# A two-layer attention kernel whose first q and k are projected from centred values and scaled as they leave PSUM

## The chip, the cores and the metric

The kernel runs on one core of a Trainium2 chip. The metric is the device time of one execution in microseconds (us), the median of several. The core has five engines that run side by side, each taking its own instructions in order: TensorE (PE, matrix products; its weight loads are shown as PEld), VectorE (DVE), ScalarE (ACT), GpSimd (POOL) and SyncE (SP, which here only issues DMAs). Products land in PSUM, [...]which this kernel holds as four tiles of two banks with the tags a, b, c and d. A tile is reused only when its readers are done.

## The reference

Sixteen images of 256 channels on a 32 by 32 grid go through two layers. Each layer normalises in 16 groups and adds the attention of the normalised image to the image:

```python
def _gn(v, G=16, eps=1e-5):
    B_, H_, W_, C_ = v.shape
    g = v.reshape(B_, H_, W_, G, C_ // G)
    m = jnp.mean(g, axis=(1, 2, 4), keepdims=True)
    s = jnp.var(g, axis=(1, 2, 4), keepdims=True)
    return ((g - m) / jnp.sqrt(s + eps)).reshape(v.shape)

...
    q = proj(Wq, bq)
    k = proj(Wk, bk)
    v = proj(Wv, bv)
    sim = jnp.einsum('bhdi,bhdj->bhij', q, k)
    rel = (rel_h + rel_w).reshape(heads, d, n)
    qpos = jnp.einsum('hdi,bhdj->bhij', rel, q)
    attn = jax.nn.softmax(sim + qpos, axis=-1)
    out = jnp.einsum('bhdn,bhmn->bhdm', v, attn)
...
x = x + _L0_conv_ref(_gn(x), ...)
x = x + _L1_conv_ref(_gn(x), ...)
```

There are 4 heads of 64 channels and 1024 positions. The groups lie along the last axis of the grid: a group is two neighbouring columns of every row of every channel. A group's mean and its 1/sqrt(variance), called rstd below, are therefore the same for all channels and differ by position only. Since a projection sums over channels, a factor that depends on the position alone can be applied to the projection's result as well as to its input.

## The kernel before

**Units and blocks.** A unit is one image in one layer, so there are 32. A unit has four blocks: two pairs of heads (`pr`) by two halves of the query positions (`half`). A block computes the scores of both heads of its pair as eight tiles `ps` of 128 keys by 2 x 512 queries (L385), their exponentials `p` (L394, on ACT), the running sum `acc` of those for the softmax's denominator (L403, L405, on DVE), and the product with the values, `po` (L419). Before PE adds the scores to a tile, DVE writes the position term there from `abt` (a "seed", L349).

**What stands between.** The function `block` writes out the order of work by hand, and a manual schedule keeps it, so each engine executes its instructions in the order in which the code names them. Between its own scores a block runs pieces of the unit's second pair and of the next unit (`prepare`): values (L298), q and k (L268), positions (L326). A projection or value product is made in two stretches; between the two stands a small write on POOL (L166) that waits for the first and releases the second.

**Normalisation ahead.** While unit u runs, the statistics of unit u + 2 are gathered on ACT in 16 groups each of sums (L190 with Identity) and squares (L190 with Square), and unit u + 1 is normalised in 16 ACT instructions (`norm_apply`, L248). A product with the constant matrix `avg` adds a statistic over the partitions: `norm_mean` and `norm_var` by four small products (L209). rstd is a power, taken on POOL (L237).

**The beginning.** Before the first block no earlier work is there to hide in. SP loads image 0, Wq and Wk of layer 0 (`raw0`), image 1, both Wv (`raw1`), Wq and Wk of layer 1 (`raw2`), the small tables and image 2. Weights are transposed on PE (L126) and copied out by ACT (L137). For image 0, DVE sums by group (L858), PE averages (L868), ACT negates the mean (L870), DVE writes the centred image `xn` (L875), ACT and DVE share the squares (L190, L888, L889), PE averages (L894), DVE adds epsilon (L896), POOL takes the power (L901), and DVE and ACT share the scaling of `xn` (L928, L925). Then PE makes q and k (L268), ACT adds the bias on the way out of PSUM (L279), PE makes the positions. Unit 1's mean and squares are made in between, all before block 0; its rstd is ready during block 0, whose `norm_apply` calls begin with it. Unit 2's sums run on ACT in blocks 0 and 1 (`norm_sums`).

**The end.** The last block makes the sums for its softmax on PE into a PSUM tile `pd`. DVE takes the reciprocal (L827), ACT copies the sums to SBUF (L829), two DMAs bring one row of each head into a table (L831), and DVE and PE reduce that table to a flag that says whether all sums were in range. The copy's buffer `d` comes from the pool of the exponentials:

```python
    d = ppool.tile([P, 2, HALF], F32, tag="p", name=f"d_{n + 1}")[:, 0, :]
    nc.scalar.copy(d, pd)
```

The four PSUM tags go round in a list `ring`, which starts as b, c, a, d.

Of the kernel before, what the change touches and what calls it, by code (L numbers as in the profile page):

```python
# [9 lines left out]
F32 = mybir.dt.float32  # L10
# [7 lines left out]
P = 128  # L18
# [34 lines left out]
def fast_path(ctx, tc, sh, x, layers, out, W, den_all, token, good, flag):  # L53
# [55 lines left out]
    def load_raw(name, parts):  # L109

        raw = ppool.tile([P, 2, HALF], F32, tag="p", name=name)
        for a, (l, part) in enumerate(parts):
            nc.sync.dma_start(
                raw[:, a, :].rearrange("p (oc c) -> p oc c", c=C),
                layers[l][part].rearrange("(oc p) c -> p oc c", p=P),
            )
        return raw, parts
# [74 lines left out]
        )  # L192

    def norm_sums(u, gs):
        if u not in reds:
            reds[u] = small.tile([P, G], F32, tag="red", name=f"red_{u}")
        for g in gs:
            of_group(u, g, AF.Identity, reds[u])
# [27 lines left out]
    def norm_squares(u, gs):  # L226
        for g in gs:
            of_group(u, g, AF.Square, sums[u], bias=negs[u][:, g : g + 1])
# [14 lines left out]
        return out_of_psum  # L243

    def norm_apply(u, gs):
        rstd, shift = rss[u]
        for g in gs:
            nc.scalar.activation(  # L248
                grouped(xns[u], g),
                grouped(xt[units[u][0]], g),  # L250
                AF.Identity,
                bias=shift[:, g : g + 1],
                scale=rstd[:, g : g + 1],
            )
# [142 lines left out]
    def add_up(blk, j):  # L397
        u, pr, half = blk
        if j == 0:
            return  # L400
        if j == 1:
            accs[blk] = apool.tile([P, 2, HALF], F32, tag="acc", name=f"acc_{u}_{pr}_{half}")
            nc.vector.tensor_tensor(accs[blk], probs[blk, 0], probs[blk, 1], ALU.add)  # L403
        else:
            nc.vector.tensor_tensor(accs[blk], accs[blk], probs[blk, j], ALU.add)  # L405
# [179 lines left out]
    BPU = CC * NH  # L585

    pos = {}
    ring = ["b", "c", "a", "d"]

    def nothing(*_):  # L590
        return None
# [1 line left out]
    def prepare(u, b):  # L593
# [22 lines left out]
            positions(u, 0, psum2(y, f"pa_{u}_0")),  # L616
        )

    def block(n):
        blk = blocks[n]  # L620
        u, b = divmod(n, BPU)
# [17 lines left out]
        if previous:  # L639
# [4 lines left out]
                add_last(previous)  # L644
            else:
                add_up(previous, 7)
        for j in range(1, 4):
            scores(blk, j)
        (first, first_out), (second, second_out) = prepare(u, b)
        first(0)  # L650
        if b == 0 and one:
            norm_apply(u + 1, range(0, 1))
        if b == 1 and two:
            norm_sums(u + 2, range(9, 11))
        seed(blk, 4, f1)
        scores(blk, 4)
        add_up(blk, 1)
        if b == 0 and one:
            norm_apply(u + 1, range(1, 5))
        if b == 1 and two:  # L660
            norm_sums(u + 2, range(11, 12))
        if b == 2 and two:
            norm_squares(u + 2, range(0, 5))
        second(0)
        if half == 1:
            second_out()
# [16 lines left out]
        if previous and folded:  # L683
            stack_up(previous)
        add_up(blk, 2)
        if half == 0:
            second(1)
            second_out()
# [10 lines left out]
            seed(after, 0, f0)  # L699
        if n in check:  # L700
            next(checks)
        if b == 0 and one:
            norm_apply(u + 1, range(5, 9))
        if b == 0 and two:
            norm_sums(u + 2, range(0, 2))
        if b == 1 and two:
            norm_sums(u + 2, range(12, G))
        if b == 1 and one:
            norm_apply(u + 1, range(9, 11))
        if b == 2 and two:  # L710
            norm_squares(u + 2, range(5, 11))
        po = psum2(ring[3], f"po_{n}")
        values_of_p = attend(blk, po)
        values_of_p(0)
# [4 lines left out]
                mean_out = norm_var(u + 2, filled(f1, f"pm_{n}", EPS / 2))  # L719
        if after:  # L720
            scores(after, 0)
        values_of_p.word()
        if stacked:
            fold_stack(*stacked, R // 2)
# [5 lines left out]
            add_up(blk, 5)  # L730
        if before:
            finish(*before)
        if two and half == 1:
            mean_out()
        if stacked:
            fold_stack(*stacked, R // 4)
# [5 lines left out]
                seed(after, j, ring[j % 3])  # L742
        if summed:
            reciprocals(*summed)
        if b == 0 and two:
            norm_sums(u + 2, range(2, 9))
        if b == 1 and one:
            norm_apply(u + 1, range(11, G))
        if b == 2 and two:
            norm_squares(u + 2, range(11, G))  # L750
        values_of_p(1)
        take_out(blk, po)
        pos[n] = po
# [8 lines left out]
    def block_without_pieces(n, half):  # L762
# [62 lines left out]
        values_of_p(1)  # L825
        rden = rdens[u, pr][:, HALF:]
        nc.vector.reciprocal(rden, pd)  # L827
        d = ppool.tile([P, 2, HALF], F32, tag="p", name=f"d_{n + 1}")[:, 0, :]
        nc.scalar.copy(d, pd)  # L829
        for hs in QUARTERS:  # L830
            nc.sync.dma_start(den_all[hs, n, :], d[hs.start : hs.start + 1, :])  # L831
# [7 lines left out]

    load_x(0)  # L840
    raw0 = load_raw("raw0", [(0, "Wq"), (0, "Wk")])
    load_x(1)
    raw1 = load_raw("raw1", [(0, "Wv"), (1, "Wv")])
    raw2 = load_raw("raw2", [(1, "Wq"), (1, "Wk")])
    W.load_rest(nc.sync, 0)
    load_x(2)
# [2 lines left out]
    def by_group(t, g0=0, g1=G):  # L849
        return t.rearrange("p c (w g t) -> p (c w) g t", g=G, t=GT)[:, :, g0:g1, :]  # L850

    def spread(t, g0=0, g1=G):
        return (
            t[:, g0:g1].unsqueeze(1).unsqueeze(3).to_broadcast([P, CC * sh.W, g1 - g0, GT])
        )

    def reduced(u, cc):
        nc.vector.tensor_reduce(  # L858
            reds[u][:, cc, :],
            xt[units[u][0]][:, cc, :].rearrange("p (w g t) -> p g w t", g=G, t=GT),  # L860
            AX.XY,
            ALU.add,
        )

    def first_mean(u, pm):
        red = reds.pop(u)
        for cc in range(CC):
            nc.tensor.matmul(pm, W.avg, red[:, cc, :], start=(cc == 0), stop=(cc == CC - 1))  # L868
        negs[u] = small.tile([P, G], F32, tag="neg", name=f"neg_{u}")
        nc.scalar.mul(negs[u], pm, -1.0)  # L870
        sums[u] = small.tile([P, G], F32, tag="sum", name=f"sum_{u}")
        xns[u] = gnpool.tile([P, CC, N], F32, tag="gn", name=f"xn_{u}")

    def centred(u, g0, g1):
        nc.vector.tensor_tensor(  # L875
            by_group(xns[u], g0, g1),
            by_group(xt[units[u][0]], g0, g1),
            spread(negs[u], g0, g1),
            ALU.add,
        )  # L880

    def rest_of_squares(u, g0):

        sq = ppool.tile([P, 2, HALF], F32, tag="p", name=f"first_sq_{u}")
        sq = sq.rearrange("p a n -> p (a n)")[:, : CC * sh.W * (G - g0) * GT].rearrange(
            "p (w g t) -> p w g t", g=G - g0, t=GT
        )
        nc.vector.tensor_tensor(sq, by_group(xns[u], g0), by_group(xns[u], g0), ALU.mult)  # L888
        nc.vector.tensor_reduce(  # L889
            sums[u][:, g0:], sq.rearrange("p w g t -> p g w t"), AX.XY, ALU.add  # L890
        )

    def first_var(u, pm):
        nc.tensor.matmul(pm, W.avg, sums.pop(u), start=True, stop=True)  # L894
        var = small.tile([P, G], F32, tag="var", name=f"var_{u}")
        nc.vector.tensor_scalar(var, pm, EPS, None, ALU.add)  # L896
        return var

    def first_rstd(u, var):
        rstd = small.tile([P, G], F32, tag="rstd", name=f"rstd_{u}")  # L900
        nc.gpsimd.tensor_tensor(rstd, var, W.mhalf[:, :G], ALU.pow)  # L901
        return rstd

    for u in range(2):
        reds[u] = small.tile([P, CC, G], F32, tag="first_red", name=f"first_red_{u}")
    G1, G2 = G // 2 + 2, G // 4
    pm0 = psum2("c", "pm_0")
    for cc in range(CC):
        reduced(0, cc)
    first_mean(0, pm0[:, 0, :G])  # L910
    transposed("a", *raw0)
    norm_squares(0, range(G1))
    centred(0, 0, G)
    rest_of_squares(0, G1)
    rstd0 = first_rstd(0, first_var(0, pm0[:, 1, :G]))
    taken(raw0[1])
    transposed("b", *raw1)
    taken(raw1[1])
    pm1 = psum2("d", "pm_1")
    for cc in range(CC):  # L920
        reduced(1, cc)
    first_mean(1, pm1[:, 0, :G])
    transposed("a", *raw2)
    for g in range(G2):
        nc.scalar.activation(  # L925
            grouped(xns[0], g), grouped(xns[0], g), AF.Identity, scale=rstd0[:, g : g + 1]
        )
    nc.vector.tensor_tensor(  # L928
        by_group(xns[0], G2), by_group(xns[0], G2), spread(rstd0, G2), ALU.mult
    )  # L930
    taken(raw2[1])
    norm_squares(1, range(0, G // 2))
    centred(1, G // 2, G)
    rest_of_squares(1, G // 2)
    (q, q_out), (k, k_out) = (
        project(0, 0, which, psum2(tag, f"p{which}_0_0")) for which, tag in (("q", "b"), ("k", "c"))
    )
    q(0)
    k(0)
    q(1)  # L940
    q_out()
    k(1)
    k_out()
    ab, ab_out = positions(0, 0, psum2("a", "pa_0_0"))
    ab(0)
    ab_out()
    var1 = first_var(1, pm1[:, 1, :G])
    for j in range(3):
        seed(blocks[0], j, ring[j])
    v, v_out = values(0, 0, psum2("d", "pv_0_0"))  # L950
    v(0)
    scores(blocks[0], 0)
    v(1)
    v_out()
    seed(blocks[0], 3, ring[0])
    rstd1 = first_rstd(1, var1)
    shift1 = small.tile([P, G], F32, tag="nshift", name="nshift_1")
    nc.vector.tensor_tensor(shift1, negs.pop(1), rstd1, ALU.mult)
    rss[1] = (rstd1, shift1)
    for n in range(len(blocks)):  # L960
        block(n)

# [279 lines left out]
```

## Time and profile before

| what | value |
|---|---|
| median of three runs | 2537.84 us (2536.82 to 2538.13) |
| the profiled execution's own time | 2537.8 us |
| its span in the profile | 2535.9 us |
| PE busy | 2512.9 us, 99% of the span |
| DVE busy | 2267.8 us, 89% |
| ACT busy | 1949.0 us, 77% |
| POOL busy | 834.1 us, 33% |

The span reaches from the first to the last instruction recorded; 1.9 us of the execution's time lie around it. A row of the profile names the line of the code, the engine, and the tiles written and read. "x16" counts instructions; a matrix product in 32-bit floats shows as two records. Times within the trace count from the start of the span.

### The profile page before, as it was taken

Reading aid. Unit: us, or ns where it says so; the run is one execution under the profiler, and the core shown is the slowest. Engines: PE = TensorE matmul, PEld = TensorE weight load, DVE = VectorE, ACT = ScalarE, POOL = GpSimd, SP = SyncE. Lnnn points to the kernel's source line nnn. Section 1 sums busy time; section 2 is a strip of 40 time slices with the busy share of each in tenths; the row PEclk is TensorE's granted clock in tenths of the full one; section 3 lists DMA queues with packets and bytes.
Section 4 is the critical chain, followed back from the end, with each engine's and each line's share of the span. In section 5 each row is a group of like instructions: output and inputs, shape, how many; then the busy total and the mean of one; then the engine's idle time right before and its main releaser. Section 6 shows DMA issues by size and latency. Waiting matters only on the chain.

```text
span 2535.9 us, 85952 instructions
## 1 busy us (share of the span) xinstructions
PE 2512.9 (99%) x37462; PEld 1332.5 (53%) x37462; DVE 2267.8 (89%) x2133; ACT 1949.0 (77%) x3876; POOL 834.1 (33%) x1195
## 2 busy tenths in 40 slices
PE   8999999999999999999999999999999999999998
PEld 4555555555555555555555555555555555555554
DVE  6898998989989989899899899998998999989997
ACT  6778777787777887777877778877778777787654
POOL 1333333323333233333233332333323333323320
PEclk9999999999999999999999999999999999999999
DMA  3344443544444445444444444444454444444442
GB/s 90 74 79 75 87 87 67 101 96 93 96 90 104 80 76 101 88 84 95 92 88 94 79 97 81 85 104 90 87 112 81 90 79 84 80 84 77 95 81 69
DMA packets 119841, 221.57 MB, mean 87 GB/s; under 512 B 53913, under 2 KB 55449, under 8 KB 119457
## 3 DMA queue, kind: packets, MB, share of 16 engines
q0 software_dynamic: 53712, 130.10, 31.4%
q1 hardware_dynamic: 65744, 85.90, 12.0%
q8 instruction: 295, 4.83, 0.8%
q14 instruction: 90, 0.73, 0.1%
HBM read 51.78 MB, written 17.30 MB: 27 GB/s over the span
## 4 chain that ended last, share of the span: by engine, by line
PE 97%; DVE 1%; DMA 1%; POOL 1%; issue 1%; SPq 0%; ACT 0%; POOLq 0%; DVEq 0%; ACTq 0%
PE ps L385 34%; PE po L419 34%; PE pk L268 9%; PE pv L298 9%; PE pq L268 9%; PE pa L326 2%; DMA stack<-stack 0%; DMA den_all<-d 0%; PE pm L209 0%; DMA x<-in_x_dram 0%; DVE acc L405 0%; DVE rden L827 0%; POOL rstd L237 0%; POOL rstd L901 0%; POOL stack L460 0%
## 5 line engine op out<-in xcount | busy, mean ns | idle before, releaser
L349 DVE TENSOR_TENSOR ps<-abt 128x1024 f32<-128x1024 f32 x1018 | 1228.8, 1230 | 230.3 <-ACT p L394 144.3
L394 ACT ACTIVATE p<-ps,shift 128x1024 f32<-128x1024 f32 x1024 | 1091.3, 1114 | 335.4 <-PE ps L385 335.4
L385 PE MATMUL ps<-q,k 64*64 64x512 f32 x8192 | 985.9, 590 | 0.0
L419 PE MATMUL po<-p,v 64*64 64x256 f32 x16384 | 930.5, 376 | 0.0
L419 PEld LDWEIGHTS po<-p,v 64*64 64x64 f32 x16384 | 629.1, 133 | 364.3 <-issue 77.2
L405 DVE TENSOR_TENSOR acc<-acc,p 128x1024 f32<-128x1024 f32 x643 | 780.4, 1214 | 8.2 <-ACT p L394 1.4
L385 PEld LDWEIGHTS ps<-q,k 64*64 64x64 f32 x8192 | 306.6, 133 | 397.9 <-issue 274.9
L166 POOL MEMSET token<- 1x1 f32 x320 | 36.2, 113 | 1033.5 <-PE po L419 469.9
L465 POOL DMA_DIRECT2D stack<-stack x310 | 255.0, 823 | 196.0 <-DMA stack<-stack 109.4
L298 PE MATMUL pv<-Wv,xn 64*64 64x256 f32 x4096 | 244.3, 376 | 0.6 <-POOL token L166 0.3
L268 PE MATMUL pq<-xn,Wq 64*64 64x512 f32 x2048 | 243.8, 591 | 0.3 <-DVE xn L928 0.3
L268 PE MATMUL pk<-xn,Wk 64*64 64x512 f32 x2048 | 242.8, 589 | 0.0
L460 POOL DMA_DIRECT2D stack<-acc x248 | 221.6, 1075 | 41.6 <-issue 30.0
L248 ACT ACTIVATE xn<-x,nshift,rstd 128x128 f32<-128x128 f32 x496 | 210.3, 496 | 1.1 <-POOL nshift L239 1.1
L298 PEld LDWEIGHTS pv<-Wv,xn 64*64 64x64 f32 x4096 | 153.5, 133 | 102.7 <-issue 51.6
L436 POOL DMA_DIRECT2D acc<-p x124 | 118.8, 958 | 247.3 <-ACT od L480 162.3
L190 ACT ACTIVATE junk<-x,neg 128x128 f32<-128x128 f32 x498 | 195.2, 400 | 0.0
L480 ACT COPY od<-po 128x512 f32<-128x512 f32 x127 | 74.3, 585 | 114.9 <-PE po L419 114.9
L403 DVE TENSOR_TENSOR acc<-p,p 128x1024 f32<-128x1024 f32 x128 | 155.8, 1217 | 0.0
L441 POOL DMA_DIRECT2D acc<-acc x124 | 106.0, 855 | 148.3 <-DMA acc<-p 139.3
L268 PEld LDWEIGHTS pq<-xn,Wq 64*64 64x64 f32 x2048 | 78.6, 134 | 142.1 <-issue 133.2
L190 ACT ACTIVATE junk<-x 128x128 f32<-128x128 f32 x480 | 145.0, 311 | 0.0
(75 smaller groups left out, 1124.5 us busy)
## 6 DMA issues: line engine op xcount, KB each, us to landing
acc<-p POOLq DMA_DIRECT2D x124, 512.0 KB, 5.7
rden<-rd SPq DMA_DIRECT2D x126, 256.0 KB, 6.0
acc<-acc POOLq DMA_DIRECT2D x124, 256.0 KB, 3.6
x<-in_x_dram SPq DMA_DIRECT2D x32, 512.0 KB, 4.3
stack<-acc SPq DMA_DIRECT2D x248, 64.0 KB, 2.1
stack<-acc POOLq DMA_DIRECT2D x248, 64.0 KB, 3.0
out_dram<-x SPq DMA_DIRECT2D x31, 512.0 KB, 3.8
stack<-stack POOLq DMA_DIRECT2D x62, 128.0 KB, 4.2
```

Source lines behind the costliest of these rows:

```text
L190: nc.scalar.activation(junk, grouped(xt[units[u][0]], g), func, accum_out=into[:, g : g + 1], **bias)
L248: nc.scalar.activation(grouped(xns[u], g), grouped(xt[units[u][0]], g), AF.Identity, bias=shift[:, g : g + 1], scale=rstd[:, g : g + 1],)
L268: yield nc.tensor.matmul(pk[c, nh, :], w[l][rs, cc, c0 : c0 + D], xns[u][rs, cc, nh * HALF : (nh + 1) * HALF], start=(t == 0 and cc == 0), ...
L298: yield nc.tensor.matmul(pv[c, a, i, :], xns[u][rs, cc, j0 : j0 + D], W.wv[l][rs, cc, :], start=(t == 0 and cc == 0 and i == 0), stop=(t = ...
L349: nc.vector.tensor_tensor(ps.rearrange("p h (w y) -> p h w y", y=H), ab[:, :, :H].unsqueeze(2).to_broadcast([P, 2, XH, H]), ab[:, :, H + h ...
L385: nc.tensor.matmul(ps[c, h, :], a[hs, j0 : j0 + D], b[hs, columns], start=bool(tag) and i == 0, stop=i == len(terms) - 1, skip_group_check ...
L394: nc.scalar.activation(p, ps, AF.Exp, bias=W.shift)
L403: nc.vector.tensor_tensor(accs[blk], probs[blk, 0], probs[blk, 1], ALU.add)
L405: nc.vector.tensor_tensor(accs[blk], accs[blk], probs[blk, j], ALU.add)
L419: yield nc.tensor.matmul(po[c, a, :QUART], vts[u][rs, j, c0 : c0 + D], p[rs, h, a * QUART : (a + 1) * QUART], start=(t == 0 and j == 0), s ...
L460: nc.gpsimd.dma_start(at, acc[R:D, h, :], accum_op=ALU.add)
L465: nc.gpsimd.dma_start(stack[:rows_], stack[rows_ : 2 * rows_], accum_op=ALU.add)
```

## The change

Six things change.

1. q and k of unit 0, first pair, are projected from the centred image. DVE multiplies by rstd as it takes them out of PSUM, in halves of 512 positions, and ACT then adds the bias in place. The product for the variance stands between the first stretches of q and k. `xn` itself is scaled later, half before the first seed and half between the third and the fourth, since the values and the second pair still read it.
2. Both Wv are loaded before image 1 and transposed right behind layer 0's Wq and Wk. The transposes of layer 1's Wq and Wk move behind the positions. The shares of the squares of image 0 shift: 9 groups on ACT and 7 on DVE, 10 and 6 before.
3. Unit 1's mean is made before block 0, its 16 squares from just before block 0 to the end of it, its variance and rstd at the end of block 0, and its 16 applications in block 1 (before: all squares ahead of block 0, 9 applications in block 0, 7 in block 1).
4. Unit 2's sums are made by DVE, one reduction in block 0 and one in block 1, in place of 16 instructions on ACT.
5. The calls for later units come from tables that name the same groups at the same four places; at the third place of a unit's first block two sums now stand before four applications.
6. The ring starts as c, a, b, d, and the last sums' copy takes its buffer from the pool of `acc`.

```diff
-    ring = ["b", "c", "a", "d"]
+    ring = ["c", "a", "b", "d"]
...
+    APPLY = {0: (0, 1, 5, 9, 9), 1: (9, 9, 9, 11, G)}
+    SUMS = {0: (0, 0, 0, 2, 9), 1: (9, 11, 12, G, G)}
+    SQUARES = {2: (0, 0, 5, 11, G)}
+
+    FIRST_SQUARES = {0: (3, 5, 9, G, G)}
+    FIRST_APPLY = {1: (0, 1, 4, 8, G)}
+
+    def norms(u, b, i):
+        def groups(table):
+            return range(*table.get(b, (0,) * 5)[i : i + 2])
+
+        if u == 0:
+            norm_squares(1, groups(FIRST_SQUARES))
+        elif u + 2 < NU:
+            norm_sums(u + 2, groups(SUMS))
+        if u + 1 < NU:
+            norm_apply(u + 1, groups(APPLY if u > 0 else FIRST_APPLY))
+        if u + 2 < NU:
+            norm_squares(u + 2, groups(SQUARES))
...
-        for j in range(1, 4):
+        for j in range(1 if n > 0 else 2, 4):
             scores(blk, j)
         (first, first_out), (second, second_out) = prepare(u, b)
         first(0)
...
+        norms(u, b, 0)
+        if n == 1:
+            reduced(2, 1)
+            added(2)
         seed(blk, 4, f1)
...
         add_up(blk, 2)
+        if n == 0:
+            reduced(2, 0)
...
         if after:
             scores(after, 0)
+        if n == 0:
+            mean_out = norm_var(1, filled(f1, f"pm_{n}", EPS / 2))
         values_of_p.word()
...
-        d = ppool.tile([P, 2, HALF], F32, tag="p", name=f"d_{n + 1}")[:, 0, :]
+        d = apool.tile([P, 2, HALF], F32, tag="acc", name=f"d_{n + 1}")[:, 0, :]
...
     load_x(0)
     raw0 = load_raw("raw0", [(0, "Wq"), (0, "Wk")])
+    raw1 = load_raw("raw1", [(0, "Wv"), (1, "Wv")])
     load_x(1)
-    raw1 = load_raw("raw1", [(0, "Wv"), (1, "Wv")])
...
+    def scaled(into, t, rstd):
+
+        shape = dict(g=G, t=GT)
+        nc.vector.tensor_tensor(
+            into.rearrange("p (w g t) -> p w g t", **shape),
+            t.rearrange("p (w g t) -> p w g t", **shape),
+            spread(rstd, XH),
+            ALU.mult,
         )
...
     transposed("a", *raw0)
...
+    transposed("b", *raw1)
+    norm_squares(0, range(4))
     taken(raw0[1])
...
+    norm_squares(0, range(4, G // 2 + 1))
+    nc.vector.tensor_tensor(
+        by_group(xns[0]), by_group(xt[0]), spread(negs[0], CC * sh.W), ALU.add
+    )
+    rest_of_squares(G // 2 + 1)
+    pq, pk = psum2("c", "pq_0_0"), psum2("a", "pk_0_0")
+    q, k = project(0, 0, "q", pq)[0], project(0, 0, "k", pk)[0]
+    q(0)
+    q.word()
+    nc.tensor.matmul(pm0[:, 1, :G], W.avg, sums.pop(0), start=True, stop=True)
+    var = small.tile([P, G], F32, tag="var", name="var_0")
+    nc.vector.tensor_scalar(var, pm0[:, 1, :G], EPS, None, ALU.add)
+    rstd = small.tile([P, G], F32, tag="rstd", name="rstd_0")
+    nc.gpsimd.tensor_tensor(rstd, var, W.mhalf[:, :G], ALU.pow)
     taken(raw1[1])
...
     for cc in range(CC):
         reduced(1, cc)
...
+    added(1)
+    pm1 = filled("d", "pm_1", 0.0)
     k(0)
     q(1)
...
     k(1)
...
+            scaled(t[:, nh * HALF : (nh + 1) * HALF], ps[:, nh, :], rstd)
...
+    biased("q", W.bq, 0)
+    biased("q", W.bq, 1)
+    biased("k", W.bk, 0)
...
+    mean_out = norm_mean(1, pm1)
+    ab, ab_out = positions(0, 0, psum2("b", "pa_0_0"))
     ab(0)
     ab_out()
...
+    biased("k", W.bk, 1)
+    mean_out()
...
+    first_scaled(0)
+    transposed("d", *raw2)
+    taken(raw2[1])
+    seed(blocks[0], 0, ring[0])
+    scores(blocks[0], 0)
+    seed(blocks[0], 1, ring[1])
+    seed(blocks[0], 2, ring[2])
     v, v_out = values(0, 0, psum2("d", "pv_0_0"))
     v(0)
...
+    norm_squares(1, range(3))
+    first_scaled(1)
+    scores(blocks[0], 1)
     v(1)
     v_out()
     seed(blocks[0], 3, ring[0])
```

`first_scaled(nh)` calls `scaled` on `xn` in place, for both halves of the channels of one half of the positions.

## The prediction

> **What bounds the kernel now.** I read four views, in this order: busy time and granted clock by stretches, the chain of waits in order of time, TensorE (PE) busy in windows of 3.41 us, and the timeline at both ends.
>
> Stretches (us from the span's start; length, then busy us and count of PE, PEld, DVE, ACT, POOL; granted clock, DMA share, GB/s):
>
> ```profile
> 0.00:18.09 18.09, 8.01 (x34) 7.04 (x35) 11.32 (x14) 9.10 (x32) 3.62 (x7) 1.00 0.68 216
> 18.09:26.20 8.11, 8.11 (x76) 3.12 (x80) 3.44 (x3) 5.10 (x19) 0.18 (x2) 1.00 0.39 120
> 26.20:35.03 8.83, 8.56 (x170) 4.91 (x165) 5.56 (x7) 5.64 (x6) 3.60 (x2) 1.00 0.01 3
> 35.03:75.00 39.97, 39.97 (x596) 20.93 (x592) 33.87 (x32) 34.13 (x72) 4.97 (x10) 1.00 0.16 28
> 75.00:2500.00 2425.00, 2424.62 (x36340) 1283.06 (x36336) 2188.22 (x2051) 1884.34 (x3739) 820.76 (x1172) 1.00 0.45 88
> ```
>
> From 35 us to 2500 us PE never rests, so there the order of its products is the time, and nothing the other engines save counts until PE waits for them. Time can be won only before about 35 us. The chain there (start, length, what):
>
> ```profile
> 1.21 4.55 DMA x<-in_x_dram
> ...
> 7.92 2.30 DVE xn L875
> ...
> 11.24 0.96 DVE sum L889
> ...
> 13.22 2.94 POOL rstd L901
> 16.16 0.02 issue
> 16.19 1.77 DVE xn L928
> 17.96 0.14 issue
> 18.09 2.99 PE pq L268 x16
> 21.09 1.72 PE pk L268 x16
> ...
> 29.72 1.01 PE ps L385 x8
> 30.73 1.73 PE pv L298 x32
> ...
> 35.03 1.73 PE pv L298 x32
> ```
>
> The first q product waits for the full normalisation: centring, squares, variance, the power on POOL (2.94), the scaling (1.77). The row at 35.03 is the second half of the values, the first product of block 0 that stands at the same place of PE's order in both kernels. It is my milestone: how much earlier does it start?
>
> **The change, part by part.** *q and k from centred values.* Centring ends at 10.21. The product at 18.09 no longer waits for the variance, the power or the scaling. What is late next is PE itself: 8 transposes of raw0 end at 9.45 (7.50 + 1.95), and the change puts the 8 of raw1 straight behind, at 0.22 each (1.76 for 8): 11.2. Their weights must be there: Wv landed 7.3 and 7.6 us after issues at 3.66 and 4.14, behind the second image's 1 MB. The change issues them before it; with about 0.7 us for each 256 KB (Wq landed at 6.6, Wk at 7.6) I get 8.3 and 9.0, in time. Wq leaves PSUM on ACT after four squares of 0.39 (7.92, 8.32, 8.71, 9.11 are the starts) and one copy, at 10.1, in time. So q starts at **11.2**, 6.9 us earlier.
>
> *The clock.* The row says x16 in 2.99 for the first q stretch and 1.72 for the next of the same form. PE windows (length, busy us, count, granted clock, DMA share, GB/s):
>
> ```profile
> 13.43:16.84 3.41, 2.92 (x15) 1.00 0.08 12
> 16.84:20.26 3.42, 3.16 (x17) 1.00 0.95 305
> ...
> 2505.16:2508.57 3.41, 0.76 (x8) 1.00 0.98 246
> ```
>
> The pace doubles at 20.26, inside the first q stretch (the 1.00 there says nothing: the pace was half of it). The window before 16.84 was 2.92 busy, mostly transposes, and did not raise it; the next, with 2.17 us of real products, did. At the end a window with 0.76 busy lowered it for 3.41 us. [...] This speaks against the change: q moves to 11.2 behind nothing but transposes, so it begins just as cold. By the row alone the loss stays 1.27 (2.99 - 1.72) and the four stretches end at 11.2 + 6.88 + 1.27; [...] I take the middle, **1.95**, since the window's phase need not repeat, and keep both ends. With the variance product now between q and k (0.4, row L894) the projections end at K = 11.2 + 6.88 + 0.40 + 1.95 = **20.4**, against 26.23.
>
> *The power on POOL* starts when that variance product is through (about 14.9) and ends at 14.9 + 0.2 + 2.94 = 18.0. q is complete at K - 1.72 = 18.7, so the power is hidden with 0.7 to spare; the reductions of image 1 (2 x 1.2) run beside it on DVE.
>
> *Scaling out of PSUM* is not in the trace. Nearest rows: the 128x512 product out of PSUM (L561, 0.69) and L928, 1.76 for 1536 elements, so 0.59 for 512. I take 0.66; ends 0.59 and 0.69, which over the four on the path is 0.4 us in all. q is scaled by K - 0.3 and biased on ACT (128x512, 0.59 like L829) by K + 0.3; the positions (0.93) begin at K with q's first half and end at K + 1.05. DVE then has in order: k scaled (2 x 0.66), unit 1's mean (0.2), half of xn scaled (2 x 0.66), the first seed (1.23): K + 4.1. The abt copy (1.00 on ACT, behind one k bias) is out at K + 2.35, hidden. The 8 raw2 transposes, which before were over by 17.8, now stand at K + 1.65 to K + 3.4, because their bank holds unit 1's mean; scores 0 follow at K + 4.15, with PE idle for 0.6 + 0.75. So scores 0 start at **24.6** against 29.72: 6.9 us have shrunk to 5.1.
>
> *To the milestone.* Behind it PE does scores 0, values, scores 1, values, scores 2 and 3: 4 x 0.86 + 2 x 1.73 = 6.9, so 31.5. The values wait for the copies of Wq1 and Wk1 (1.07 behind the transposes): K + 4.5, which scores 0 hide with 0.5 to spare. **31.5 against 35.03 is 3.5 us.**
>
> *Unit 1's variance in blocks 0 and 1.* ACT in block 0 before: 9 applications at 0.42 and 9 sums at 0.31, 6.6 us; after: 13 squares at 0.39, 5.1. Block 1 before: 7 and 7, 5.1; after: 16 applications, 6.7. Unit 2's 16 sums go to DVE as two reductions of 1.2, one in each block. In the stretch 35 to 75, two blocks long, ACT and DVE have 5.8 and 6.1 us free, so +1.6 on ACT and +1.4 on DVE in block 1 fit on the whole but not at each place: three applications (1.3) stand before the copy of abt, which frees the bank of seed 7, and DVE comes to that seed 1.4 later. Walking block 1 leaves PE 0.35 late at scores 7. Ends 0 and 1.6; I take **0.35**. The new variance product at the end of block 0 waits for all 16 squares: scores 7 end at 31.5 + 10.3 = 41.8, exp 1.15, seven squares 2.75, so 45.9; PE arrives at 31.5 + 14.65 = 46.15. Hidden by 0.2 us.
>
> *Rest.* Unit 1's DMA lands about 1.4 us later (11.75), DVE asks at 15.1. The ring only renames banks. In later units the one difference is two sums ahead of four applications, on an ACT with 1884 of 2425 us busy and no reader before the next block: nothing. The last sums:
>
> ```profile
> 2522.49 3.36 DVE L827 RECIPROCAL rden<-pd 128x512 f32<-128x512 f32 x1
> 2525.94 0.58 ACT L829 COPY d<-pd 128x512 f32<-128x512 f32 x1 [7.50 <-DVE rden L827]
> ```
>
> The copy waits for the reciprocal that reads the same PSUM tile, and the other buffer leaves that wait as it is: 0 (ends -0.1 and +0.1).
>
> **Sum.** 3.53 - 0.35 = 3.2. The span was 2535.9 and the run 2537.8, 1.9 around it, next to the median of 2537.84; so span 2532.7 and time **2534.6**, 0.13% faster. A difference under 0.2% (5.1 us) can hardly be told from none here.
>
> **Rivals.**
> 1. *The clock is up early.* If transposes do count towards it (16.84 to 20.26 was 3.16 busy with them) the clock rises between 11.2 and 13, the loss is 0 to 0.9 instead of 1.95, and with no stall in block 1 (0.35) the middle is 1.9 better: 2532.7. Against it: the 2.92 window.
> 2. *The clock falls again.* Between K and scores 0 PE has the positions (0.93) and transposes alone for 4.1 us. If a window falls there and positions or transposes count little, the next 3.41 us run at half pace: 1.7, so 2536.3. For it: the 0.76 window; against: with the positions the emptiest window has about 1.0.
> 3. *Slower: ACT falls behind in blocks 0 and 1.* The cover at unit 1's variance product is 0.2, and PE waits in order behind it. If the accumulator reads (0.19) don't hide behind the squares, 13 x 0.2 = 2.6; applications at their mean of 0.50 give 16 x 0.08 = 1.3; with the 1.6 at block 1's copies that is 5.5, less the 3.2: 2540.1. It decides from 3.2 us of ACT lateness. Against: the squares' starts, 0.39 apart in the trace.
> 4. *The change does not do what it says:* q waits for the power all the same. Then K is 18.0 plus the products, near 26, and the time 2538. The order of PE's products excludes it nearly.
>
> **How the numbers follow.** Likeliest 0.62 (2533.2 to 2536.0 from the clock's ends and the stalls); rival 1 0.20; rival 2 0.12; rival 3 0.05; rival 4 0.01. Range 2532.5 to 2537.2. Faster by over 0.2% is time below 2532.8: half of rival 1 and a tenth of the likeliest, 0.15; slower by over 0.2%, over 2542.9, only if rival 3 is worse than priced: 0.03; within: 0.82.
>
> **What would show it.** q's first row near 11.2 with a length of 2.8 to 3.5; the power ending before q's second stretch; scores 0 near 24.6 and the milestone near 31.5; an idle of PE before scores 7 of block 1 below 1 us; the row before the last sums' copy still naming the reciprocal. Wrong would be: a wait on ACT squares at the end of block 0, a low-clock stretch after 23, or a milestone later than 33.

## The result and the profile after

The changed kernel takes **2531.26 us** (median of 13 runs, 2530.43 to 2533.23), the kernel before in the same set of runs 2537.64 (13 runs, 2536.55 to 2538.55). The ratio is 0.9975, 95% interval 0.9968 to 0.9983. So the change gains 6.4 us, about twice what was predicted, and the time lies 1.2 us below the range. The profiled execution's span is 2529.2 us, 6.7 shorter than before. The prediction had put a gain of more than 0.2% at a chance of 0.15; it was 0.25%.

First the stretches of the changed kernel, with the columns of the table of before. The first three cuts are at the same events: first q product, end of the projections, milestone (the second half of the values in block 0). The fourth is block 2's first q product, 68.99 here and 73.94 in the kernel before, whose table cuts at 75.00; the last is 2495.

```profile
0.00:10.81 10.81, 4.54 (x21) 4.20 (x21) 5.83 (x8) 4.54 (x15) 0.69 (x6) 1.00 0.82 300
10.81:18.39 7.58, 7.58 (x77) 2.81 (x78) 5.41 (x9) 3.31 (x12) 3.08 (x3) 1.00 0.47 124
18.39:29.36 10.97, 9.45 (x179) 5.82 (x176) 10.57 (x13) 8.74 (x16) 0.09 (x1) 1.00 0.23 65
29.36:68.99 39.63, 39.53 (x597) 20.44 (x592) 33.47 (x35) 32.63 (x65) 8.85 (x12) 1.00 0.16 29
68.99:2495.00 2426.01, 2425.62 (x36346) 1284.67 (x36342) 2190.55 (x2052) 1885.51 (x3740) 822.44 (x1173) 1.00 0.45 88
```

The second row is the surprise of the first half: all four projection stretches and the variance product fit into 7.58 us of PE, where the prediction had 9.2. The chain of waits (start, length, what) says why:

```profile
10.88 1.88 PE pq L268 x16
12.75 0.33 PE pm L926 x2
13.08 1.88 PE pk L268 x16
14.96 1.72 PE pq L268 x16
16.67 1.71 PE pk L268 x16
...
19.84 1.20 DVE xn L864 x2
21.04 1.16 DVE ps L349
22.20 0.04 issue
22.24 1.09 PE ps L385 x8
...
29.36 1.73 PE pv L298 x32
```

The first q stretch is 1.88 us long where before it was 2.99: PE is already close to its later pace of 1.72 (the k stretch behind the variance product takes 1.88 as well). The milestone stands at 29.36, 5.67 earlier than the 35.03 of before (forecast: 31.5, 3.53 earlier).

The way from the milestone to the end holds two more differences. The same place in block 2, its first q product, is 68.99 after and 73.94 before: 4.95, so 0.72 is lost in blocks 0 and 1. The last product with the values (`po`, L419) ahead of the chain of DMAs that sets the end starts at 2472.18 after and 2477.13 before, still 4.95: in between nothing is won or lost, as was expected of a stretch in which PE hardly rests (2425.62 of 2426.01 us busy in the last row of the table). But `flag`, the last result, is done at 2523.05 after and 2530.28 before, 7.23 earlier. **So 2.28 us were won in the last 53 us**, where the prediction had put nothing. After the flag 0.54 is lost again (6.20 to the end of the span against 5.66); I didn't follow that; the 13 profiles have 5.66 to 6.24 there, and e3, which leaves the start alone, 6.05. Together: 5.67 - 0.72 + 2.28 - 0.54 = 6.7.

What happened near the end? The chain of waits of the kernel before, and then of the changed one:

```profile
2483.73 2.65 DMA stack<-stack
2486.66 3.23 DMA stack<-stack
...
2508.00 0.14 DVE range L568
2508.14 1.55 PE po L490 x8
```

```profile
2478.80 2.71 DMA stack<-stack
2481.79 2.17 DMA stack<-stack
...
2502.10 0.14 DVE range L568
```

`stack<-stack` (L465) is a DMA that folds a stack of partial softmax sums in half; three small folds follow each other, 32, 16 and 8 KB. The last takes 3.23 us before and 2.17 after. Everything behind it on DVE comes later by the difference, and PE waits for DVE in front of the products at L490, by the timeline of PE, before and after:

```profile
2508.14 1.55 PE L490 MATMUL po<-acc,ones 128*32 128x256 f32 x8 [2.65 <-DVE range L568]
```

```profile
2502.25 1.06 PE L490 MATMUL po<-acc,ones 128*32 128x256 f32 x8 [1.90 <-DVE range L568]
```

Before, the longer rest makes a window with 0.76 us of PE work, which the prediction showed, and the granted clock is 0.50 in the next window (length, PE's busy us and count, granted clock, DMA share, GB/s):

```profile
2508.55:2511.97 3.42, 3.42 (x19) 0.50 0.33 67
```

In the changed kernel the emptiest window there is this one, and its clock stays up:

```profile
2498.94:2502.35 3.41, 1.51 (x18) 0.45 (x12) 3.31 (x5) 2.86 (x3) 0.00 (x0) 1.00 1.03 241
```

What held up the fold? The DMA queues in a short window across it (queue and kind, packets, MB, share of 16 engines); first before, 2487.6 to 2488.9, then after, 2481.7 to 2482.8:

```profile
q0 software_dynamic: 32, 0.01, 6.0%
q8 instruction: 1, 0.02, 5.4%
```

```profile
q8 instruction: 1, 0.02, 5.5%
```

The 32 packets on q0 are the fold. The one packet on q8 is 16 KB of instruction code (16,384 bytes in its record). Before, both are under way together: the code from 2487.67 to 2488.80, the fold's packets from 2488.04 to 2488.81. After, the code arrives alone, and the fold's packets come 0.46 us after it is through. The page counts 295 such packets in the changed kernel (4.83 MB), beside 74,944 recorded instructions of PE (37,472 product records and as many weight loads). If all of them are PE's code, which no view says, one packet holds some 254 instructions; from this estimate I count by 256 below. My theory was that where one of them falls goes by how many PE instructions the program has up to there; the experiments below test it.

### The profile page after: what moved, and what is told of

It is laid out like the page before. It is cut to its first block, busy times and chain, and to the rows that moved or that the text cites. A ratio compares the mean times of both kernels' runs of the same rounds, so it can differ in the third digit from the quotient of the medians.

```text
span 2529.2 us, 85968 instructions
## 1 busy us (share of the span) xinstructions
PE 2508.5 (99%) x37472; PEld 1331.3 (53%) x37472; DVE 2270.3 (90%) x2143; ACT 1945.5 (77%) x3855; POOL 836.1 (33%) x1196
## 3 DMA queue, kind: packets, MB, share of 16 engines
q0 software_dynamic: 53712, 130.10, 31.5%
q8 instruction: 295, 4.83, 0.8%
## 4 chain that ended last, share of the span: by engine, by line
PE 96%; DVE 2%; DMA 1%; issue 1%; POOL 0%; SPq 0%; ACT 0%; DVEq 0%; POOLq 0%
PE po L419 34%; PE ps L385 34%; PE pv L298 9%; PE pk L268 9%; PE pq L268 9%; PE pa L326 2%; DVE ps L349 1%; DVE acc L405 0%; PE pm L209 0%; DMA den_all<-d 0%; DMA stack<-stack 0%; DMA x<-in_x_dram 0%; DVE acc L403 0%; PE raw_t L126 0%; POOL rstd L237 0%
## 5 line engine op out<-in xcount | busy, mean ns | idle before, releaser
L419 PE MATMUL po<-p,v 64*64 64x256 f32 x16384 | 930.6, 376 | 0.0
L419 PEld LDWEIGHTS po<-p,v 64*64 64x64 f32 x16384 | 629.6, 133 | 363.1 <-issue 77.2
L465 POOL DMA_DIRECT2D stack<-stack x310 | 254.9, 822 | 189.5 <-DMA stack<-stack 103.6
```

What stands on the lines that cost most here:

```text
L419: yield nc.tensor.matmul(po[c, a, :QUART], vts[u][rs, j, c0 : c0 + D], p[rs, h, a * QUART : (a + 1) * QUART], start=(t == 0 and j == 0), s ...
L465: nc.gpsimd.dma_start(stack[:rows_], stack[rows_ : 2 * rows_], accum_op=ALU.add)
```

## The experiments

The theories were: beyond the forecast the start gains through the clock, because the transposes of both Wv behind those of Wq and Wk fill PE and the clock rises before q; and the end gains because the place of PE's code loads moved. The rivals: the start gains in another way, the end gains through the copy's other buffer, or through the shorter start. The recorded expectations letter their theories A, B and C anew for each run.

**e1_same: the change once more.**

> The changed kernel again, for a second profile. Theory A (transposes count towards the clock, so the sixteen back to back raise it before q): the first q stretch takes 1.7 to 1.9 us whatever the phase of the window, or at most 1.0 longer where a window ends early among them. Theory B (the phase of the window happened to be kind in the first profile): the stretch takes 2.2 to 3.5 in most profiles. Both: 6.4 us under the kernel before. For the end: if the 2.3 us won behind block 120 are a matter of the window's phase and of one DMA, this profile has another length there; if they belong to the change, the same 50.9 us from the last products of block 123 to the flag.

2531.20 us (9 runs), ratio 0.9974 (0.9964 to 0.9984). The clock rises at 11.27, inside the q stretch (2.04 long in the timeline, 1.95 in the first profile), L490 is waited for 1.77 us, no low clock at the end. Both gains repeat. The q stretch fits neither of the two theories cleanly: over more profiles its length varies (see the clock, below).

**e2_busy: the kernel before, with PE kept busy by transposes ahead of q.**

```diff
     transposed("a", *raw0)
+    busy = psum2("d", "busy")
+    for i in range(12):
+        nc.tensor.transpose(busy[:, 0, i % 4 * P : (i % 4 + 1) * P], W.ident, W.ident)
```

> The kernel before with twelve transposes of the identity put into PE's idle time behind raw0 (9.5 to 12.2 us), into a PSUM tile that nobody reads. They change nothing but how busy PE is. Theory A: the clock is up before q, its first stretch takes 1.7 to 1.9 instead of 2.99, q still starts near 18; the time falls by 1.1 to 2.0 us. Theory B: transposes do not count, the time stays (within 0.4) and the first stretch stays at 2.2 to 3.5.

The q stretch didn't shorten: 3.69 us. Three windows of PE in this run tell the reason (two with the columns of the stretches, the last with PE's alone):

```profile
8.28:11.69 3.41, 3.41 (x18) 3.27 (x16) 3.34 (x3) 3.41 (x18) 0.00 (x0) 1.00 1.06 366
11.69:15.10 3.41, 1.85 (x14) 1.37 (x12) 2.86 (x4) 2.21 (x6) 2.15 (x1) 1.00 0.32 45
15.10:18.52 3.42, 3.09 (x14) 0.50 0.46 123
```

The first is full, all of it transposes, and PE's pace nearly doubles at its end, 11.69: eight transposes take 1.95 us from 7.45 and 1.07 from 12.50. The second has 1.85 us of transposes and small products, and from 15.10 to 21.93 the granted clock is 0.50. q comes at 17.83, in between. So here a window of transposes alone brought the full pace, and it was lost again behind a window with 1.85 us of work, before q came; in the changed kernel q follows the transposes at 10.81, and the windows from 10.64 to 17.47 are full. The time was 2536.25 (13 runs), ratio 0.9994 (0.9985 to 1.0002): nothing that can be told from none, and in the profile a loss at the start with a gain at the end. The 12 transposes had moved the code loads too (table below), so this run is no clean measure of the clock alone.

**e3_buffer: the kernel before, with the last sums' copy from the pool of `acc`.**

```diff
-        d = ppool.tile([P, 2, HALF], F32, tag="p", name=f"d_{n + 1}")[:, 0, :]
+        d = apool.tile([P, 2, HALF], F32, tag="acc", name=f"d_{n + 1}")[:, 0, :]
```

> The kernel before with the last sums' copy in the other pool's buffer, that part of the change alone. My forecast: 0, within 0.3 us, the copy still waiting for the reciprocal. Rival: the buffer is what shortened the end, 1 to 2.3 us less.

2537.66 (13 runs), ratio 1.0000 (0.9992 to 1.0009). The last fold is 3.60, the wait 2.65, the low clock is there. The chain shows the copy behind the reciprocal as before:

```profile
2523.11 3.32 DVE rden L827
2526.45 0.59 ACT d L829
```

The buffer alone is worth nothing, and the end's gain isn't its doing.

**e4_gap: the change, with the transposes of both Wv moved behind the first q stretch.**

```diff
     transposed("a", *raw0)
-    transposed("b", *raw1)
...
     nc.gpsimd.tensor_tensor(rstd, var, W.mhalf[:, :G], ALU.pow)
+    transposed("b", *raw1)
```

> The changed kernel with raw1's eight transposes moved behind the first q stretch and the variance product, so that PE has only eight transposes before q and idles from about 9.3 until Wq is copied at about 9.9. Theory A: q starts near 10.0 at half clock, its stretch takes 2.8 to 3.5, k follows 1.8 later for the transposes; 1.0 to 2.5 us over the changed kernel. Theory B: q starts 0.8 earlier with a clock no worse than before, so at most 0.8 over the changed kernel.

2533.63 (21 runs), ratio 0.9984 (0.9977 to 0.9990): 2.4 above the change. Timeline of PE:

```profile
7.59 1.95 PE L126 MATMUL raw_t<-ident,raw 128*128 128x128 f32 x8
10.45 3.27 PE L268 MATMUL pq<-xn,Wq 64*64 64x512 f32 x16 [0.90 <-DVE xn L917]
13.64 0.40 PE L925 MATMUL pm<-sum,avg 128*128 128x16 f32 x2
13.88 1.07 PE L126 MATMUL raw_t<-ident,raw 128*128 128x128 f32 x8
```

With a rest of 0.90 ahead of it, q starts even earlier, and takes 3.27: the clock rises only at 13.15, and at 10.64 in the change. Eight transposes of one form cost 1.95 ahead of that point and 1.07 behind it. The order of the transposes is what brings the clock up in time; this is what the start won beyond the forecast.

**e5_moved and e6_moved: only the place of PE's code.** The kernel before with 12 tiny products at the start (48 recorded instructions), and the change with 59 of them (236), so many that its code stands at the same place, counted by 256 and within one, as that of the kernel before.

```diff
+    moved = psum2("a", "moved")
+    for i in range(12):
+        nc.tensor.matmul(moved[:16, 0, :16], W.ones[:, :16], W.ones[:, :16], start=True, stop=True)
     pm0 = psum2("c", "pm_0")
```

> The kernel before with twelve tiny products (16 columns by 16) in PE's idle time ahead of image 0, into a PSUM tile that nobody reads. All later PE instructions stand 48 places further on in its code. Theory C (a 16 KB load of PE's code falls on the last fold of the sums by DMA near the end, 7 us after that chain begins, and makes it 3.2 to 3.6 us long; PE then rests 2.65 and its clock drops for a window; the change only moved the load away): the load comes 1.2 us earlier, the fold takes 2.2, PE rests 1.8, the clock stays up, and the time falls by 1.0 to 2.3 us, with the beginning unchanged. Rival (the end is shorter because of what the change does to it): within 0.4 of the kernel before.

2537.97 (13 runs), ratio 0.9999 (0.9991 to 1.0008): this expectation was missed. The chain shows where the load went:

```profile
2484.29 4.25 DMA stack<-stack
...
2488.81 2.17 DMA stack<-stack
```

The last fold is fast now, and the one ahead of it slow: 4.25 in place of 2.65. The load had been moved from one fold to the one ahead of it, and PE waits 2.65 all the same.

> The changed kernel with 59 of those tiny products ahead of image 0, which puts PE's code at the same place within its 16 KB pieces as in the kernel before (20 places back, less a whole piece). Theory C: the fold takes 3.2 to 3.6 again, PE rests about 2.6, the clock may drop for a window; 1.0 to 2.3 us over the changed kernel. Rival: within 0.4 of the changed kernel. Either way the beginning stays as it is.

2534.82 (21 runs), ratio 0.9986 (0.9979 to 0.9993): 3.6 above the change, or 3.1 when each is set against the kernel before of its own set. That is more than was expected, and the start, which was to stay as it is, didn't: the milestone is 30.34, 1.0 later than in the change. The last fold takes 3.79, PE waits 2.65, the clock is low for 6.83 us, and the end alone, from that last product with the values to the flag, is 4.2 longer. The profile, at 2536.16, is one of the slowest of the 21 runs, so the loss at the end of a typical run is probably smaller than that.

**e9_moved5: the kernel before with five tiny products** (20 recorded instructions), so that its code stands where that of the change does, within one. The diff is that of e5 with 5 for 12.

> The kernel before with five tiny products at the start, so that its instructions of PE near the end stand at the same place of their code as in the changed kernel. Theory A (the end's gain is the load of PE's code, which no longer falls on a fold of the sums): the third fold takes about 2.2 us where the kernel before had 3.2, PE's wait before the last products is about 1.8 in place of 2.65, no low-clock window follows, and the time is 1.0 to 2.3 us below the kernel before. Rival (the end's gain needs the rest of the change): within 0.5 us of the kernel before, fold near 3.2, wait 2.65.

2536.12 (13 runs), beside 2537.91 for the kernel before in the same set: -1.8, as its theory A said; the ratio is 0.9993 with an interval of 0.9984 to 1.0001, which by itself just includes no change. The profile decides it. Chain of waits, and PE's windows across the rest:

```profile
2484.46 2.59 DMA stack<-stack
...
2487.32 2.17 DMA stack<-stack
```

```profile
2503.32:2506.73 3.41, 2.71 (x28) 0.97 (x20) 3.34 (x4) 2.96 (x4) 0.68 (x1) 1.00 0.61 156
2506.73:2510.14 3.41, 2.67 (x24) 1.16 (x25) 3.34 (x6) 1.33 (x2) 0.00 (x0) 1.00 0.71 156
```

The fold is fast, the rest 1.44 us, and it falls across two windows that keep 2.7 us of work each. From the last product with the values to the flag this kernel takes 50.54 us, before 53.15, the change 50.87. Its span is only 1.7 shorter than before, since the first q stretch took 3.69 in place of 2.99. Nothing of the change is in it but the place of the code.

All profiles side by side. "Code" is how many recorded instructions of PE stand ahead of that last product more than in the kernel before, counted by 256 (a transpose shows as one product record and one weight load); "load" is when the code's packet starts, from POOL's go-ahead for the first of the three folds; "low clock at the end" leaves out the last fall, which lasts to the end of the span (from 2529.05 before and 2522.85 in the change); "end" is the time from that last product to the flag:

| kernel | code | load, us | slow fold, us | PE's rest, us | low clock at the end, us | end, us |
|---|---|---|---|---|---|---|
| e6_moved | -1 | 7.33 | third, 3.79 | 2.65 | 6.83 | 55.09 |
| before | 0 | 6.93 | third, 3.23 | 2.65 | 3.41 | 53.15 |
| e3_buffer | 0 | 7.44 | third, 3.60 | 2.65 | 3.41 | 53.16 |
| after | +19 | 5.95 | none | 1.90 | 0 | 50.87 |
| e1, e4, e7, e8, e10, e11 | +19 | 5.72 to 5.89 | none | 1.43 to 1.95 | 0 | 50.48 to 51.00 |
| e9_moved5 | +20 | 5.72 | none | 1.44 | 0 | 50.54 |
| e2_busy | +25 | 5.75 | none | 1.83 | 0 | 50.92 |
| e5_moved | +48 | 5.19 | second, 4.25 | 2.65 | 3.41 | 53.13 |

The further the code is moved, the earlier the load comes: from the third fold (0 and -1) into the pause between the two (+19 to +25) and on to the second (+48). At one place it still varies by 0.5 us (6.93 and 7.44), so the number says roughly where a load falls. e6 stands 255 records on from the place of before (19 and 236), and its load is back near that of before (7.33 and 6.93): this agrees with the estimate of some 254 to a packet. In all four profiles with a slow fold the clock fell for 3.41 us or more; in the other nine PE's products behind the rest keep the full pace (1.06 us for the eight of L490, 1.06 to 1.11 for each eight of the next 32), where in these four a group of eight reaches 1.99 to 2.01 us. In the slow fold of before the packet trace shows the contact itself: the fold's last two packets, of 8 and 4 bytes, end at 2488.81, within 0.02 us of the end of the code's packet at 2488.80, when its other packets have been through for 0.3 us.

**e7, e8, e10, e11: the stall in block 1.** The tables of waits show one wait of PE for a seed, of 1.2 us, and I took it for scores 7 of block 1. All four expectations carry this mistake. The timeline puts that wait ahead of scores 0, at 22.24, where it is a part of the start; in block 1 PE's loss is smaller and is spread inside a row of 24 product records, which take 2.75 us without a stall. e7 moves DVE's second reduction for unit 2 to block 0, e8 moves it behind the last seed, e10 moves ACT's first four applications behind the copy of `abt`, e11 is e7 and e10 together:

```diff
-    FIRST_APPLY = {1: (0, 1, 4, 8, G)}
+    FIRST_APPLY = {1: (0, 0, 0, 8, G)}
...
-        if n == 1:
-            reduced(2, 1)
-            added(2)
...
             reduced(2, 0)
+            reduced(2, 1)
+            added(2)
```

> The changed kernel with both of DVE's reductions for unit 2 in block 0. If DVE's reduction ahead of seed 4 in block 1 is what made PE wait 1.2 us at scores 7, that wait goes and 0.5 to 0.9 us with it, unless block 0 now waits for seeds in its place (then 0 to +0.5). If it is the three applications on ACT before the copy of abt, the wait stays and the time is within 0.3.

> The changed kernel with DVE's second reduction for unit 2 in block 1 behind the last seed instead of ahead of seed 4. As for the run with both in block 0: 0.5 to 0.9 us less if that reduction's place makes the wait at scores 7, within 0.3 if ACT's applications do.

> The changed kernel with the first eight of unit 1's 16 applications behind the copy of the second pair's positions in block 1, in place of three ahead of it. Theory A (PE's 1.2 us wait before scores 7 of block 1 comes from the three applications on ACT ahead of the copy that frees seed 7's bank): the wait falls below 0.4 us and the time is 0.5 to 0.9 below the changed kernel. Rival (DVE's second reduction holds the seeds): the wait stays above 0.8 and the time is the same within 0.4.

> The changed kernel with both edits: the eight applications behind the copy and both of DVE's reductions for unit 2 in block 0. Theory A (ACT alone): as e10 within 0.3 us, wait below 0.4. Rival (both engines hold the seeds, one behind the other): the wait goes only here, 0.6 to 1.0 us below e10.

The row of scores 5 to 7 in block 1, by the timeline, for the change, e10 and e11 in turn:

```profile
55.34 3.19 PE L385 MATMUL ps<-q,k 64*64 64x512 f32 x24
```

```profile
56.69 3.13 PE L385 MATMUL ps<-q,k 64*64 64x512 f32 x24
```

```profile
55.98 2.75 PE L385 MATMUL ps<-q,k 64*64 64x512 f32 x24
```

0.44 us too long in the change, 0.38 with the applications moved, 0 with both (one profile each). With the reduction moved alone (e7, e8) the loss stays 0.44, by the distance to the next row; e8 adds another wait of 0.37 for a PSUM tile that DVE clears. So **both engines hold the last seed, one as late as the other**: the theory that ACT alone does it fell, and so did DVE alone. The times are 2531.69 (e7, 12 runs), 2532.08 (e8, 11), 2531.73 (e10, 9) and 2531.17 (e11, 9), ratios 0.9977, 0.9977, 0.9977 and 0.9975. The 0.44 us that e11 wins in its profile is lost among the starts: its clock rises at 11.69, one us later than in the profile of the change. e11 and the change can't be told apart, and no run beat them.

## Why the prediction was wrong, step by step

**The clock, 1.95 us: the term that failed first.** The 1.95 was my estimate, and no view of before shows it; the one loss that its trace shows is 1.27 (2.99 - 1.72). I assumed that transposes don't count towards the clock, and used the window of 2.92 us before 16.84 as the evidence. The window ahead of q in the changed kernel is full:

```profile
7.23:10.64 3.41, 3.41 (x18) 3.35 (x17) 2.87 (x2) 3.08 (x13) 0.00 (x0) 1.00 1.04 396
```

3.31 of it are transposes, 0.10 a small product, and the clock is up at 10.64, before q. The measurement decides against my assumption. Why the 2.92 window failed stays open: 2.23 of it were transposes, and e4 has one of 2.70, all of it q, which sufficed, while a full window of transposes was enough in this profile and in e2. Whether transposes count less than products was not shown. The loss was at most 0.16 (1.88 - 1.72) in place of 1.95, and since the k stretch also takes 1.88 with the clock long up, even that may not be the clock.

Part of this is luck. The phase of the window shifts from run to run: in six profiles that start like the change (the change, e1, e7, e8, e10, e11) the clock rose at 10.64, 11.27, 11.91, 12.58, 13.28 and 11.69, and the q stretch was 1.95, 2.04, 2.40, 2.70, 3.00 and 2.17 long, on average 0.43 more than the first, so for a typical run the term would be about 0.6. The profile of before was the kindest of its kind too: in four that start like it the stretch was 2.99, 3.47, 3.67 and 3.69. From the profile of before to that of the change the stretch shortened by 1.04, from mean to mean by 1.08. Rival 1 named this mechanism and gave it 0.20; with its 1.9 us it would have been the better forecast.

**The end, nothing in the sum: the larger omission.** I wrote that time can be won only before 35 us, since PE never rests until 2500, and priced nothing of the end but the copy's buffer. I had shown the 0.76 window that lowers the clock near the end, and didn't ask what makes PE rest there, and whether that would stay. It was a fold slowed by a code load (3.23 us against 2.17), and with the 19 records more that the change has up to there the load came at 5.95 in place of 6.93 us, off the fold; in e9 20 records alone did it (5.72). 2.28 us; together with the clock's 1.79 this is more than the miss. The range had room for an early clock (rival 1's 2532.7); no rival and no end of a range had room for this.

**What held.** q started at 10.88 (forecast 11.2; 0.32 better, with Wv there in time). The power on POOL ran from 13.38 to 16.31 and q's scaling began at 16.82, when PE was through: hidden by 0.5 (forecast 0.7). The scaling out of PSUM, which the trace of before did not have, is in DVE's timeline now:

```profile
16.82 1.29 DVE L864 TENSOR_TENSOR q<-pq,rstd 128x512 f32<-128x512 f32 x2 [0.97 <-PE pq L268]
18.46 1.29 DVE L864 TENSOR_TENSOR k<-pk,rstd 128x512 f32<-128x512 f32 x2 [0.35 <-PE pm L209]
```

0.65 each (forecast 0.66). Scores 0 followed 3.85 behind the projections (forecast 4.15; the scaling of `xn` took 0.60 a piece and not 0.66, the seed 1.16). Rival 2 didn't come: the window from 20.88 to 24.29 was 2.16 busy, and the clock stayed up. Rival 3 didn't come at the end of block 0 either: the 16 squares were out at 43.86, and PE reached the product at 43.99, so the cover was 0.1 (forecast 0.2, but the terms written there add up to 45.7 and not 45.9, a cover of 0.45). The last sums' buffer was 0, as forecast. Rival 4 is excluded.

**Blocks 0 and 1, 0.35:** 0.44 at scores 7, of the size and at the place given. The 0.72 lost there holds another 0.28 for unit 1's variance product, which before stood ahead of the milestone; I had asked whether it would wait, and forgot to count the product itself.

**The sum against the profile.** 3.2 was forecast for the span, 6.7 measured. The difference of 3.5: clock 1.79, q's start 0.32, scores 0 sooner behind the projections 0.30, small remainders up to the milestone -0.27, blocks 0 and 1 -0.37, the end 2.28, behind the flag -0.54.

## What to carry to other kernels

Where a chain of small DMAs sets the end, look at the instruction queue beside it: here a fold with a packet of code beside it was 1.5 to 1.75 times as long (3.23 to 3.79 us against 2.17, 4.25 against 2.65), and 20 more recorded instructions at the start of PE's code moved that packet's start from 6.93 to 5.72 us (e9). Before an end's gain is credited to an edit, run the old kernel with a few dummy instructions.

To have the clock up when the first real products start, try all work that PE can do early, transposes included, in one piece right ahead of them. Here sixteen transposes in one piece ahead of q had it up at 10.64 to 13.28 us, during q or before it; eight of them moved behind q, with a rest of 0.9 us in their place, cost 2.4.

A row in a table of waits names a line, not an occurrence: find its time before building a theory on it.

## What the runs showed of the hardware

- The recorded changes of PE's granted clock lie whole multiples of 3.4133 us apart: 20.26, 2508.57, 2511.99 and 2529.05 in the profile of before (729, 1 and 5 of them), 10.64 and 2522.85 in that of the change (736).
- A 3.41 us window full of 32-bit transposes was followed by full pace in two profiles: from 10.64 in the change (3.31 of the window transposes, the rest a small product) and from 11.69 in e2 (all transposes). So was one of 2.70, all of it q (e4, 13.15). One of 2.92, 2.23 of it transposes, was not (before, 16.84).
- Windows with 0.76, 0.83 and 1.14 us of PE work were followed by a granted clock of 0.50 (before, e3, e5), windows with 1.51, 1.64 and 2.16 were not (the change, e1, the change). But one with 1.85 us of transposes and tiny products in e2 was: busy time alone doesn't part these windows, and whether such work counts less stays open.
- A fold of 8 or 16 KB with a 16 KB packet of code beside it took 1.1 to 1.7 us longer (3.23 to 3.79 against 2.17, 4.25 against 2.6), though the code itself took only 1.13 us of one of the 16 DMA engines in before and 0.96 in the change. In before the fold's last packets end with the code's, and its landing follows them by 1.08 us; in the change the third fold, without such contact, lands 0.32 us after its last packet. Why is open.
- 8 transposes of 128x128 take 1.95 us at half pace and 1.07 at full pace (e4). The granted clock is shown as 1.00 for both, since the record of the clock begins at its first rise (20.26 in before, 10.64 in the change).
